# Blocks of 128 columns, paired writes of the transposed adjacency, and the last columns of eleven row tiles listed later

## The chip, the cores and the metric

The kernel runs on one core of one Trainium2 chip. The metric is the device time of one execution in microseconds; several runs of the same kernel are given by their median. The profile shows one execution, engine by engine: TensorE (PE, with its weight loads PEld), VectorE (DVE), ScalarE (ACT), GpSimd (POOL) and SyncE (SP), which here only starts DMAs.

## The reference

Four graph layers run one after the other on 2708 nodes with 128 features each. All use the same adjacency matrix `adj`, 2708 x 2708 in f32, symmetric in its pattern and with 0.6% of its entries other than zero; the diagonal is never zero. Every layer computes `x = x + layer(relu(layernorm(x)), adj)`.

```python
# layer 0
msg = adj.T @ h;  out = msg / adj.sum(axis=0)[:, None]
# layer 1
s, d = h @ W1[:, :D].T, h @ W1[:, D:].T
messages = gelu(s[:, None, :] + d[None, :, :] + msg_b)
aggregated = einsum('ijd,ij->id', messages, adj)
out = layernorm(gelu(concat([h, aggregated]) @ upd_w.T + upd_b) + h)
# layer 2: gru_cell(relu((adj @ h) @ W_msg.T + b_msg), h)
# layer 3: attention over the entries of adj, two heads
```

Layer 1 needs the message of a pair (i, j) only where `adj[i, j]` isn't zero. So the kernel makes lists of the nonzero entries of `adj`, and layer 1 works on the lists. Layers 2 and 3 need `adj` transposed (`adjT`), which is written to DRAM during layer 0.

## The kernel before, in words

**Tiles.** Rows are cut into 22 row tiles of 128 (the last has 20 rows), and these into six groups (`GROUPS`: five of four tiles, one of two). For layer 0 the columns are cut the same way into six column chunks c = 0 to 5. Chunks 0 to 4 have 512 columns of their own, the last (`LAST` = 5) has 148. A pair (c, s) of a column chunk and a row group is called a cut.

**Layer 0.** A loop goes through the 30 cuts of chunks 0 to 4, chunk after chunk and group after group within each (`order`). For each cut,

- `load_cut` (L320) loads the rows of the group from `adj` on SP's queue into one of five buffers `a` (`RING`). The load of the cut five places on is issued once the products of the cut have read its buffer. The last chunk has buffers `z0` to `z5` of their own, which are loaded during chunk 3.
- `list_cut` makes the lists on DVE. Columns are cut into blocks of `JB` = 124, 22 in all, the last with 104 columns. For each row tile and block, L360 finds the 8 largest values of each row, and L362 their column numbers in the block: one unit of work. A chunk's blocks 4c to 4c+3 begin at column 496c, so its window (`window`) begins before the chunk's own columns and is 512, 528, 544, 560 and 576 columns wide, and 228 for the last chunk.
- `mask_near` prepares on POOL the blocks that meet the diagonal (`near_blocks`, two of each row tile): L342 copies the block and L343 sets its diagonal to zero, since the entry on the diagonal is treated elsewhere.
- `work_cut` takes the four column tiles of the chunk in turn. For each, PE transposes the four row tiles (L406), ACT copies the result from PSUM to a buffer `aT` (L411, which sums the degrees on the way), and ACT's queue starts the write of the buffer of the turn before to `adjT` (L368, `write_one`; 128 rows of 512 columns, 256 KB). Then PE multiplies a row tile with the features (L392, `products`). `aT` has six buffers of 512 columns.

Between the cuts stand the small steps that turn the sums of earlier chunks into features of layer 1 (`turn_sums`, `turn_rows`, `destinations`, `add`, `measure`, `lift`; L255, L265, L435, L453, L464 and others). The parts of the last chunk are worked within chunk 4 (`PARTS`), and their lists (`list_last`) are spread: tiles 0 to 7 within chunk 4, tiles 8 to 13 after the last cut and ahead of `ends` (L635), tiles 14 to 16 ahead of `add(LAST)`, and tiles 17 to 20, of which only near blocks are listed here, among the steps ahead of layer 1.

**The lists that are made late.** For row tiles 17 to 20 (`LATER` to `NT - 2`) all but the near blocks, 80 units, are listed in layer 1's loop (`late_blocks`, `AT_ONCE` = 5 a period). The last row tile is listed there in a form of its own (`load_wide`, `list_wide`).

**Layer 1.** `period(t)` is executed for t = 0 to 22, with six steps k in each. PE multiplies the selected rows with selection matrices (L931, L935) and collects the results with the matrices `put` (L956); DVE prepares selection matrices (`columns`, L870 and L874; `select_rows` L776, `finish_rows` L787) and, in even periods, the sums for later tiles (`sources`, L900). At k = 4 SP issues the loads of the late blocks of the next period (`load_late`, into one of two buffers `cols_a`); at k = 1 DVE lists the first two (`EARLY`), at k = 5 the other three (`list_late`). The next period's steps follow behind these on DVE's queue.

The order of instructions on each engine is the order in which the program issues them. Waits between engines are derived from the buffers, and DMAs of SP and ACT take their semaphores from a common set in turn.

## Time and profile before

| what | value |
| --- | --- |
| time, median of 3 runs | 1015.22 us (1012.13 to 1015.25) |
| profiled execution | 1009.63 us |
| its span, first to last instruction | 1007.8 us |
| mean granted TensorE clock | 0.957 |
| PE busy | 912.5 us, 91% of the span |
| DVE busy | 795.9 us, 79% |
| ACT busy | 530.3 us, 53% |
| POOL busy | 461.4 us, 46% |
| read from DRAM, written | 117.26 MB, 30.87 MB |
| adjT writes of 256 KB on ACT's queue | 105 |

The busy time of an engine is the time in which it executed something. The shares are means over four layers that have different limits, so the page's slices (the span in 40 equal parts, each digit a busy share in tenths) are read first, then windows of the stage in question. The view of waits tells which engine stood still, which operation it was about to start, and what released it; a wait for several things is put down to the one that came last. A row of "DMA a<-in_adj" is a load of the adjacency into the ring of buffers, "adjT<-aT" a write of its transpose. Layer 0 fills the span up to about 200 us, the passage to layer 1 goes to about 245 us, and the first periods of layer 1's loop begin at about 250 us; period 1 begins at 262 us.

### The profile page before, as it was taken

What the parts mean: (1) busy time and instruction counts of PE and PEld (TensorE: products, weight loads), DVE (VectorE), ACT (ScalarE), POOL (GpSimd) and SP (SyncE); (2) the same over time, 40 slices, a digit from 0 to 9 for tenths busy, and PEclk for the clock granted to TensorE, in tenths of its full rate; (3) what the DMA queues carried; (4) which work ended last, traced back from release to release, by engine and by line L of the source; (5) the groups of instructions that cost most, each with busy time, mean ns of one, the idle gap of its engine ahead of it and who ended that gap; (6) DMA issues with size and microseconds to landing.
All of it is one profiled execution on the core that took longest, in us unless ns stands there. A gap on an engine that the chain in (4) does not pass through costs nothing. (4 is left out here: it accounts for less than half of the span.)

```text
span 1007.8 us, 22141 instructions
## 1 busy us (share of the span) xinstructions
PE 912.5 (91%) x7948; PEld 742.8 (74%) x7948; DVE 795.9 (79%) x2753; ACT 530.3 (53%) x1561; POOL 461.4 (46%) x588
## 2 busy tenths in 40 slices
PE   6799889945999999999999999999889999999983
PEld 3455455624999999999899744444678999999972
DVE  7999896976787898989966555676588977997793
ACT  5756557734666667667666324332322653564342
POOL 6413222424996779797966354443211300430142
PEclk9999999955999999999999899999899999999996
DMA  9999999422344334333322356654301574456000
GB/s 329 287 340 333 340 368 327 167 70 88 124 160 152 109 111 142 112 128 116 125 84 93 122 204 216 235 190 159 105 22 56 173 250 139 158 176 218 6 17 15
DMA packets 80458, 165.41 MB, mean 164 GB/s; under 512 B 9760, under 2 KB 25748, under 8 KB 80338
## 3 DMA queue, kind: packets, MB, share of 16 engines
q1 hardware_dynamic: 60358, 131.77, 39.7%
q10 hardware_dynamic: 19980, 32.14, 8.8%
q8 instruction: 64, 1.05, 0.4%
q14 instruction: 56, 0.46, 0.1%
HBM read 117.26 MB, written 30.87 MB: 147 GB/s over the span
## 5 line engine op out<-in xcount | busy, mean ns | idle before, releaser
L843 POOL TENSOR_SCALAR put<-count,line,value 128x128 f32<-128x128 f32 x176 | 199.7, 1146 | 10.9 <-PE agg L956 7.0
L1239 PE MATMUL att<-hv,wt 128*128 128x129 f32 x1672 | 196.0, 278 | 7.6 <-DVE wt L1209 6.2
L1239 PEld LDWEIGHTS att<-hv,wt 128*128 128x128 f32 x1672 | 192.2, 194 | 10.7 <-DVE wt L1209 8.7
L931 PE MATMUL p_m<-s,sel 128*128 128x128 bf16 x1452 | 162.3, 220 | 6.9 <-ACT g L943 4.6
L935 PE MATMUL p_m<-d,cols 124*128 124x128 bf16 (+1 forms) x1452 | 162.3, 220 | 3.9 <-DVE cols L874 3.9
L1209 DVE SCALAR_TENSOR_TENSOR wt<-row,lift,mask 128x1024 f32<-128x1024 f32 (+1 forms) x132 | 138.8, 1082 | 22.9 <-PE att L1239 22.9
L121 POOL TENSOR_TENSOR n_r<-n_r,minus_half 128x4 f32<-128x4 f32 (+1 forms) x28 | 39.6, 1413 | 243.5 <-DVE n_r L120 238.4
L956 PE MATMUL agg<-put,g 128*128 128x128 f32 (+1 forms) x968 | 123.5, 280 | 0.0
L392 PE MATMUL sums<-a,h 128*128 128x512 f32 x220 | 115.8, 622 | 1.6 <-ACT h L137 1.6
L956 PEld LDWEIGHTS agg<-put,g 128*128 128x128 f32 x968 | 114.2, 193 | 0.0
L406 PEld LDWEIGHTS p_T<-ident,a 128*128 128x128 f32 (+1 forms) x440 | 54.7, 144 | 77.1 <-issue 34.7
L931 PEld LDWEIGHTS <-sel 128*128 128x128 bf16 x1452 | 103.8, 98 | 8.6 <-issue 7.9
L1400 PE MATMUL p_agg<-a,hs 128*128 128x512 f32 (+2 forms) x264 | 107.7, 549 | 2.1 <-DMA a<-adjT 2.1
L935 PEld LDWEIGHTS <-cols 124*128 124x128 bf16 (+1 forms) x1452 | 102.8, 98 | 4.9 <-DVE cols L874 4.9
L943 ACT ACTIVATE g<-p_m 128x512 f32<-128x512 f32 x132 | 72.8, 553 | 59.4 <-PE agg L956 42.8
L852 ACT ACTIVATE put<-mine,value 128x128 f32<-128x128 bf16 x308 | 100.8, 393 | 0.0
L406 PE MATMUL p_T<-ident,a 128*128 128x128 f32 (+1 forms) x440 | 71.3, 283 | 24.6 <-ACT aT L411 18.0
L411 ACT ACTIVATE aT<-p_T 128x512 f32<-128x512 f32 (+2 forms) x132 | 71.0, 541 | 27.0 <-PE p_T L406 10.8
L1400 PEld LDWEIGHTS p_agg<-a,hs 128*128 128x128 f32 (+1 forms) x264 | 47.1, 191 | 49.2 <-issue 45.5
L362 DVE FIND_INDEX8 col<-val,a 128x8 uint16<-128x124 f32 x306 | 82.4, 281 | 0.0
L1362 ACT ACTIVATE hs<-hs 128x1354 f32<-128x1354 f32 (+1 forms) x44 | 58.4, 1329 | 39.5 <-DMA hs<-in_adj 39.1
L360 DVE MAX8 val<-a 128x8 f32<-128x124 f32 x306 | 70.9, 273 | 2.2 <-DMA a<-in_adj 2.2
(291 smaller groups left out, 1561.0 us busy)
## 6 DMA issues: line engine op xcount, KB each, us to landing
hs<-in_adj SPq DMA_DIRECT2D x42, 677.0 KB
adjT<-aT ACTq DMA_DIRECT2D x105, 256.0 KB
a<-adjT SPq DMA_DIRECT2D x20, 1280.0 KB
spread<-passed SPq DMA_DIRECT2D x22, 704.0 KB
later<-sel SPq DMA_DIRECT2D x22, 616.0 KB
a<-in_adj SPq DMA_DIRECT2D x5, 1152.0 KB
a<-in_adj SPq DMA_DIRECT2D x5, 1120.0 KB
a<-in_adj SPq DMA_DIRECT2D x5, 1088.0 KB
```

What stands on the lines that cost most here:

```text
L362: nc.vector.max_index(col[0:m, n, b, :], val[0:m, n, b, :], v)
L392: nc.tensor.matmul(accs[c][:, 0:w], h0[0:m, n, :], a[0:m, n - g0, t0 * P - lo : t0 * P - lo + w], start=(n == 0), stop=(n == NT - 1),)
L406: nc.tensor.transpose(p[0:k, i * iw + q * P : i * iw + q * P + m], a[0:m, q, e : e + k], ident[0:m, 0:m])
L843: nc.gpsimd.tensor_scalar(st["put", 0][:, b, :], count, st["line"][:, b : b + 1], st["value"][:, b : b + 1], ALU.is_equal, ALU.mult,)
L852: nc.scalar.activation(st["put", 1][:, b - HP, :], st["mine"][:, b - HP, :], AF.Identity, scale=st["value"][:, b : b + 1])
L931: nc.tensor.matmul(p[:, b - b0, :], st["sel"][:, b, :], s3[:, q, t % 2, :], start=(q == 0), stop=False)
L935: nc.tensor.matmul(p[:, b - b0, :], st["cols"][0:kb, b, :], d3[0:kb, b, q, :], start=False, stop=(q == 2))
L943: nc.scalar.activation(g[:, 0:n, :], state[t].pop(("p", k))[:, 0:n, :], AF.Gelu)
L956: nc.tensor.matmul(agg, g[:, b - 4 * k, :], put, start=(b == 0), stop=False)
L1209: nc.vector.scalar_tensor_tensor(wt[:, 0:n], row[:, k, c : c + n], lift[:, j, k : k + 1], mask[:, j, c : c + n], op0=ALU.max, op1=ALU.mult,)
L1239: nc.tensor.matmul(banks[s // 3][:, s % 3, :], wt[:, q * P : (q + 1) * P], hv[:, j, k, :], start=(v < 2 and s // 3 not in touched), stop=( ...
L1400: nc.tensor.matmul(pa[:, 0:n], h[0:k, j, :], a[0:k, j - j0, 0:n], start=(j == 0), stop=(j == NT - 1))
```

## The change

- Blocks are 128 columns wide. There are 22 still; the last has 20 columns. Windows are a chunk's own columns: 512, and 148 for the last. Each row tile has a single near block, its own (b = n), and `mask_near` has one multiply for it, on the cuts of the diagonal only.
- `late_blocks` leaves out b = n alone, which makes 84 units; the first four of them are cut off again (they are blocks 0 to 3 of tile 17, and are listed in layer 0), so 80 are left.
- The last 148 columns (blocks 20 and 21) of row tiles 6 to 16 (`HELD` to `LATER - 1`) are no longer listed in layer 0. `load_late` loads those of tile n for period n - 5, so in periods 1 to 11, with one more DMA of 128 x 148, and `list_late` at k = 5 lists them behind the other three units. The lists of tiles 0 to 5 are made in chunk 4: tiles 0 to 3 at group 1, tiles 4 and 5 at group 2. The two runs of `list_last` around `ends` and `describe` go, and of those among the steps ahead of layer 1 the two for tiles 20 and 21 are left, at the end.
- The parts of the last chunk share three buffers `z` in turn, in place of six. They are loaded at groups 3, 4 and 5 of chunk 3 and at groups 2 and 3 of chunk 4 (the last two together).
- A buffer `aT` holds 1024 columns, and there are five. The columns of two turns go into one buffer and are written with one DMA of 512 KB; parts of the last chunk, and the last row group, put as many into one as fit. A write is started, as before, at the next turn.

```diff
--- before.py
+++ after.py
@@ -41,7 +41,7 @@
 MASKED = -1e30
 FMAX = 3.4028234663852886e38
 
-JB = 124
+JB = P
 NB = (N + JB - 1) // JB
 S = 8
 E = P
@@ -192,11 +192,10 @@
     EARLY = 2
     WIDE = 4
 
-    def near_blocks(n):
-
-        return range(n * P // JB, (n * P + size(n) - 1) // JB + 1)
-
-    late_blocks = [(n, b) for n in range(LATER, NT - 1) for b in range(NB) if b not in near_blocks(n)]
+    late_blocks = [(n, b) for n in range(LATER, NT - 1) for b in range(NB) if b != n]
+    late_blocks = late_blocks[len(late_blocks) % AT_ONCE :]
+    HELD = 6
+    LAST_AT = {n - HELD + 1: n for n in range(HELD, LATER)}
     nc.gpsimd.memset(val[:, NT - 1, :, :], 0.0)
     nc.gpsimd.memset(col[:, NT - 1, :, :], 0.0)
 
@@ -285,7 +284,6 @@
 
     RING = 5
     BEHIND = 2
-    WINDOW = CH + 16 * (len(GROUPS) - 2)
     l0, ending = ExitStack(), ExitStack()
     ordered = ExitStack()
     lastp = ending.enter_context(tc.tile_pool(name="l0z", bufs=1, side="right"))
@@ -293,7 +291,7 @@
     once0 = l0.enter_context(tc.tile_pool(name="l0h", bufs=1))
     pool = l0.enter_context(tc.tile_pool(name="l0k", bufs=2))
     marked = l0.enter_context(tc.tile_pool(name="l0n", bufs=8))
-    turned = l0.enter_context(tc.tile_pool(name="l0t", bufs=6))
+    turned = l0.enter_context(tc.tile_pool(name="l0t", bufs=5))
     sump = l0.enter_context(tc.tile_pool(name="l0p", bufs=3, space=PSUM))
     turnp = l0.enter_context(tc.tile_pool(name="l0q", bufs=3, space=PSUM))
     h0 = once0.tile([P, NT, D], F32, name="h0")
@@ -305,16 +303,16 @@
 
     def window(c):
 
-        return 4 * JB * c, min(CH * (c + 1), N)
+        return CH * c, min(CH * (c + 1), N)
 
     def load_cut(c, s):
 
         g0, gk = GROUPS[s]
         lo, hi = window(c)
         if c < LAST:
-            a = rows_a.tile([P, 4, WINDOW], F32, name="a")
+            a = rows_a.tile([P, 4, CH], F32, name="a")
         else:
-            a = lastp.tile([P, gk, hi - lo], F32, name=f"z{s}")
+            a = lastp.tile([P, 4, hi - lo], F32, bufs=3, name="z")
         cuts[c, s] = a
         if gk == 4 and (c, s) != (0, 0):
             nc.sync.dma_start(
@@ -330,20 +328,13 @@
         g0, gk = GROUPS[s]
         lo = window(c)[0]
         a = cuts[c, s]
-        for n in range(g0, g0 + gk):
+        for n in range(g0, g0 + gk if c == s else g0):
             m = size(n)
-            for b in near_blocks(n):
-                if b // 4 != c:
-                    continue
-                e, k = b * JB, width(b)
-                e0, e1 = max(n * P, e), min(n * P + m, e + k)
-                p = lastp if c == LAST else marked
-                v = nears[n, b] = p.tile([P, JB], F32, name=f"near{n}_{b}" if c == LAST else "near")
-                nc.gpsimd.tensor_copy(v[0:m, 0:k], a[0:m, n - g0, e - lo : e - lo + k])
-                nc.gpsimd.tensor_tensor(
-                    v[0:m, e0 - e : e1 - e], a[0:m, n - g0, e0 - lo : e1 - lo],
-                    offdiag[0:m, e0 - n * P : e1 - n * P], ALU.mult,
-                )
+            p = lastp if c == LAST else marked
+            v = nears[n] = p.tile([P, JB], F32, name=f"near{n}" if c == LAST else "near")
+            nc.gpsimd.tensor_tensor(
+                v[0:m, 0:m], a[0:m, n - g0, n * P - lo : n * P - lo + m], offdiag[0:m, 0:m], ALU.mult
+            )
 
     def list_cut(c, s, n):
 
@@ -351,9 +342,9 @@
         lo = window(c)[0]
         units = []
         for b in range(4 * c, min(4 * c + 4, NB)):
-            if b in near_blocks(n):
-                units.append((b, nears.pop((n, b))[0:m, 0 : width(b)]))
-            elif n < LATER:
+            if b == n:
+                units.append((b, nears.pop(n)[0:m, 0:m]))
+            elif (n, b) not in late_blocks and n < (HELD if c == LAST else NT - 1):
                 units.insert(0, (b, cuts[c, s][0:m, n - GROUPS[s][0], b * JB - lo : b * JB - lo + width(b)]))
         for k in range(0, len(units), 2):
             for b, v in units[k : k + 2]:
@@ -396,6 +387,7 @@
 
         todo = list(range(g0, g0 + gk))
         js = list(range(t0, t0 + tk))
+        held = []
         turns = [js[q : q + 2] for q in range(0, tk, 2)] if gk < 4 == tk else [[j] for j in js]
         for js in turns:
             p = turnp.tile([P, CH], F32, name="p_T")
@@ -406,15 +398,21 @@
                     nc.tensor.transpose(
                         p[0:k, i * iw + q * P : i * iw + q * P + m], a[0:m, q, e : e + k], ident[0:m, 0:m]
                     )
-            aT = turned.tile([P, CH], F32, name="aT")
+            if not held:
+                aT = turned.tile([P, 2 * CH], F32, name="aT")
             for i, j in enumerate(js):
+                at = (len(held) + i) * iw
                 nc.scalar.activation(
-                    aT[0:k, i * iw : (i + 1) * iw], p[0:k, i * iw : (i + 1) * iw], AF.Copy, accum_out=degs[0:k, j, s : s + 1]
+                    aT[0:k, at : at + iw], p[0:k, i * iw : (i + 1) * iw], AF.Copy, accum_out=degs[0:k, j, s : s + 1]
                 )
             write_one()
-            written.append((
-                adjT[0:k, js[0] : js[0] + n, i0 : i0 + iw], aT[0:k, 0 : n * iw].rearrange("p (j i) -> p j i", j=n)
-            ))
+            held += js
+            if k < P or size(js[-1] + 1) < P or (len(held) + n) * iw > 2 * CH or js[-1] == t0 + tk - 1:
+                j, n = held[0], len(held)
+                written.append((
+                    adjT[0:k, j : j + n, i0 : i0 + iw], aT[0:k, 0 : n * iw].rearrange("p (j i) -> p j i", j=n)
+                ))
+                held = []
             for _ in range(2 if c == 0 else 1):
                 next(steps, None)
             if c > 0 and todo and gk == 4:
@@ -561,15 +559,17 @@
                 if c > 0 and s == (2 if c < LAST - 1 else 1) and n == g0 + 1:
                     invert(c - 1)
                 list_cut(c, s, n)
-            if c == LAST - 1 and 0 < s < LAST:
-                for n in range(2 * s - 2, 2 * s):
+            if c == LAST - 1:
+                for n in {1: range(4), 2: range(4, HELD)}.get(s, ()):
                     list_last(n)
         if i + 1 < len(order):
             mask_near(*order[i + 1])
         if i > BEHIND and i - 1 - BEHIND + RING < len(order):
             load_cut(*order[i - 1 - BEHIND + RING])
-        if c == LAST - 2:
-            load_cut(LAST, s)
+        for z in {(LAST - 2, 3): (0,), (LAST - 2, 4): (1,), (LAST - 2, 5): (2,), (LAST - 1, 2): (3,), (LAST - 1, 3): (4, 5)}.get(
+            (c, s), ()
+        ):
+            load_cut(LAST, z)
         if c > 0 and s == (2 if c < LAST - 1 else 1):
             turn_sums(c - 1)
         if (c, s) == (LAST - 1, LAST):
@@ -630,15 +630,11 @@
         split(*values_of(t), rest)
         describe_columns(t)
 
-    for n in range(8, 14):
-        list_last(n)
     nc.vector.tensor_copy(*ranked)
     for t in range(2):
         describe(t, d_rest[:, 2 * t : 2 * t + 2, :].rearrange("p q d -> p (q d)")[:, 0 : NB * S].rearrange(
             "p (b s) -> p b s", s=S
         ))
-    for n in range(14, 17):
-        list_last(n)
     add(LAST)
     measure(LAST)
     for _ in lift(LAST - 1):
@@ -710,7 +706,9 @@
             units = late_blocks[(t - 1) * AT_ONCE : t * AT_ONCE] if t > 0 else []
             if not units:
                 return
-            cols = work.tile([P, AT_ONCE, JB], F32, name="cols_a")
+            wide = N - LAST * CH
+            flat_cols = work.tile([P, AT_ONCE * JB + wide], F32, name="cols_a")
+            cols = flat_cols[:, 0 : AT_ONCE * JB].rearrange("p (b e) -> p b e", e=JB)
             state["late", t] = []
             for i, (n, b) in enumerate(units):
                 state["late", t].append((n, b, cols[0 : size(n), i, 0 : width(b)]))
@@ -728,6 +726,11 @@
                         adj[n * P : (n + 1) * P, b * JB : (b + k) * JB].rearrange("p (b e) -> p b e", e=JB),
                     )
                 i += k
+            if t in LAST_AT:
+                n = LAST_AT[t]
+                ends_of = flat_cols[:, AT_ONCE * JB :]
+                nc.sync.dma_start(ends_of, adj[n * P : (n + 1) * P, LAST * CH : N])
+                state["late", t] += [(n, NB - 2, ends_of[:, 0:JB]), (n, NB - 1, ends_of[:, JB:wide])]
 
         def list_late(t, first, last):
             units = state.get(("late", t), [])[first:last]
@@ -740,7 +743,8 @@
         pieces = [(b, min(WIDE, NB - 1 - b)) for b in range(0, NB - 1, WIDE)]
 
         def load_wide():
-            cols = state["wide"] = work.tile([P, AT_ONCE, JB], F32, name="cols_a")
+            cols = work.tile([P, AT_ONCE * JB + N - LAST * CH], F32, name="cols_a")
+            cols = state["wide"] = cols[:, 0 : AT_ONCE * JB].rearrange("p (b e) -> p b e", e=JB)
             for i, (b, k) in enumerate(pieces):
                 nc.sync.dma_start(
                     cols[i * TAIL : (i + 1) * TAIL, 0:k, :],
@@ -1114,7 +1118,7 @@
                 for g, step in updates.pop((t, k), ()):
                     update(g, step)
                 if k == GB - 1:
-                    list_late(t, EARLY, AT_ONCE)
+                    list_late(t, EARLY, None)
                     if now and NT - 2 <= t + 4 < NT:
                         count_rows(t + 4)
 
@@ -1132,12 +1136,12 @@
 
         puts = ExitStack()
         for step, n in (
-            (spread_ends, 0), (select_rows, 0), (rows, 5), (measure, 4), (turn_rows, 5), (list_last, 17),
+            (spread_ends, 0), (select_rows, 0), (rows, 5), (measure, 4), (turn_rows, 5),
             (finish_rows, 0), (fetch_both, 0), (spread_ends, 1), (select_rows, 1), (rows, 4),
-            (split_destinations, 3), (turn_rows, 4), (place, 0), (destinations, 4), (pass_on, 0), (list_last, 18),
+            (split_destinations, 3), (turn_rows, 4), (place, 0), (destinations, 4), (pass_on, 0),
             (finish_rows, 1), (fetch_both, 1), (split_destinations, 4), (destinations, 5), (spread_ends, 2),
             (select_rows, 2), (sources, 0), (sources_rest, 0), (describe_next, 2), (columns, 0), (place, 1), (split_destinations, 5),
-            *((list_last, n) for n in range(19, NT)),
+            (list_last, NT - 2), (list_last, NT - 1),
             (close_lists, 0),
         ):
             step(n)
```

## The prediction

> **What bounds the kernel now.** I began with the page's 40 slices (25.2 us each) to see where TensorE is not full.
>
> ```profile
> PE   6799889945999999999999999999889999999983
> DVE  7999896976787898989966555676588977997793
> PEclk9999999955999999999999899999899999999996
> DMA  9999999422344334333322356654301574456000
> ```
>
> Slices 1 to 7 are layer 0: DMA is at 9 and PE at 6 to 9. Slices 9 and 10 are the passage to layer 1: little DMA, half clock. From slice 11 PE is at 9. The change touches layer 0, the passage and the loop of layer 1 (to about 490 us), so I cut those open. Columns: length, busy time and count of PE, PEld, DVE, ACT, POOL, granted clock, DMA share, GB/s.
>
> ```profile
> 100.00:110.00 10.00, 7.67 (x33) 3.93 (x32) 10.00 (x65) 5.45 (x27) 1.27 (x1) 0.94 0.93 351
> 140.00:150.00 10.00, 9.12 (x41) 4.73 (x38) 7.79 (x52) 4.00 (x17) 2.94 (x5) 1.00 1.05 386
> 150.00:160.00 10.00, 8.30 (x34) 4.22 (x35) 1.44 (x11) 7.68 (x38) 3.64 (x9) 1.00 1.01 352
> 170.00:180.00 10.00, 10.00 (x67) 7.72 (x66) 10.00 (x69) 8.19 (x31) 3.31 (x9) 1.00 0.58 219
> ...
> 200.00:210.00 10.00, 7.96 (x21) 3.81 (x20) 5.54 (x32) 3.25 (x13) 2.21 (x6) 0.54 0.10 32
> ```
>
> Column chunks 1 to 3 (50.3 to 158.4 us by the last product of each) have DMA full; DVE is full but for about 14 us, most of it at 150 to 160, where it had no data. In chunk 4 (from 160) PE is full. What starves them is seen in the waits of 50 to 160 us (who waits, for whom: total, times, longest):
>
> ```profile
> SPq L320 <- PE sums L392: 65.8, 16, 7.1
> PEld p_T L406 <- ACT aT L411: 23.9, 24, 3.2
> PE p_T L406 <- ACT aT L411: 10.9, 9, 2.3
> ACT aT L411 <- DMA a<-in_adj: 8.5, 3, 3.8
> ACT junk L255 <- DMA a<-in_adj: 7.8, 3, 4.4
> ACT part_x L464 <- DMA a<-in_adj: 7.0, 2, 3.8
> ACT aT L411 <- DMA adjT<-aT: 5.7, 5, 3.2
> ```
>
> It is a ring. A load on SP waits for the products of five cuts earlier; PE waits for ACT to empty its transposes; ACT waits for a *load* of adj that its own operation doesn't read. ACT also issues the adjT writes (L368), and the loads and writes go round a small set of semaphores: a write stands behind the load that used its semaphore last. ACT stood still so for 11 gaps, 27.2 us in all, before 200 us (for instance 164.26 to 166.99, until the load issued at 158.4 landed), and 5.7 us for a write buffer.
>
> In the loop of layer 1 (262 to 404 us, then 418 to 470, same columns):
>
> ```profile
> 262.00:404.00 142.00, 141.74 (x2069) 140.36 (x2067) 120.12 (x319) 94.89 (x293) 115.15 (x122) 1.00 0.41 133
> ...
> 418.00:470.00 52.00, 50.83 (x747) 50.15 (x745) 47.09 (x144) 35.34 (x108) 44.89 (x47) 1.00 0.35 117
> ```
>
> PE bounds it; DVE has 22 us to spare in 142.
>
> **The change part by part.** The sum is made against the profiled execution: 1009.63 us, span 1007.8, 1.8 around it. It lies 5.6 us under the median of the runs, 1015.22; I carry my difference over to the median.
>
> *Load bytes.* Windows shrink from 512/528/544/560/576 and 228 columns to 512 and 148: 16+32+48+64+80 = 240 columns x 2708 x 4 B = 2.6 MB fewer. Some 2.4 MB of that falls in chunks 1 to 3, and the last columns of groups 3 to 5 (0.7 MB) load in chunk 4 instead, whose DMA share was 0.53 to 0.58. Before, 110 us moved
>
> ```profile
> DMA packets 22087, 38.02 MB, mean 346 GB/s; under 512 B 1515, under 2 KB 6015, under 8 KB 22074
> ```
>
> or 37.4 MB in 108.1 us; 34.3 MB are left. At the same 346 GB/s: 99.1 us, 9.0 less.
>
> *Paired adjT writes.* Four writes of 256 KB a cut become two of 512 KB. A round of eight semaphores, which five transfers a cut (one load, four writes) used up in 1.6 cuts, lasts 2.7 cuts, so a write is behind a load issued some 14 us ago and not 8. As built, about 27 writes of chunks 1 to 4 follow a load on its semaphore before and 16 after. I expect half or more of the 27 us of ACT stalls gone, and the stream fuller. How much rate does that give? In the 40 slices of that window the rate ran from 230 to 411 GB/s, and was low where one direction ran alone. The page "DMA: Bandwidth & Descriptors" of the Trainium skill (Bandwidth, "Where 436 GB/s comes from") says that transfers between HBM and SBUF are held by HBM at about 358 GB/s for a core: 34.3 MB then take 95.8 us, 12.3 less, and nothing more is to be had. The row above it, 386 GB/s over 10 us, contradicts that as a cap on reads and writes together; 375 would give 91.5 us, 16.6 less. What decides is therefore another engine. The buffers are 5 of 4 KB a partition for 6 of 2 KB: ten turns for six, but freed in pairs and later. If the pairs stall ACT as the single ones did (5.7 us), nothing is lost against now; that is why I don't book more than the following.
>
> *DVE in chunks 1 to 3.* From the lines by shape in the same 110 us:
>
> ```profile
> L362 DVE FIND_INDEX8 col<-val,a 128x8 uint16<-128x124 f32 x185 | 49.7, 280 | 0.0
> L360 DVE MAX8 val<-a 128x8 f32<-128x124 f32 x183 | 42.3, 271 | 2.2 <-DMA a<-in_adj 2.2
> ```
>
> A block costs about 0.445 us on DVE. Their number hardly changes here, and 4 columns more add some 8 ns a block (estimate, in proportion to the columns): 208 x 0.008 = 1.7 us. DVE was busy 96.0 of the 110 us; 97.7 after, 96 on the 108.1: so at most 12 less. PE's own work there is about 90. Three limits, 99.1 (bytes at the old rate), 96 (DVE), 91.5 (rate): I take 97, **-11**. Chunk 0 writes pairs too, but waits for its first loads: 0 to -2, I take -1. Chunk 4 is PE's pace (5.2 us a cut of its own work) and moves along: 0.
>
> *POOL.* One multiply for each diagonal tile replaces copies (0.29 us, 43 of them) and multiplies on two blocks a tile. POOL was busy 0 to 6.7 us of every 10: 0; not worth more, since nothing waited over 0.5 us for these.
>
> *Passage.* Before L635, DVE ran the lists of tiles 8 to 13, 194.15 to 199.26: 5.1 us, and PE (L453) waited 1.5 us for L635. They go. PE also arrives earlier, so not all 1.5 is won: -1. At 204.93 to 207.48 lists 14 to 16 stood before the addition of the last sums, while the last product ended at 205.8: -1.5 of 1.7. At 242.75, two near blocks of four less before the row selection: -0.5 of 0.9. Then the clock. It fell to half from 200.89 to 241.85, so the last cut's transposes and products took 1.97+4.08 us, against 2.18 for as many rows at full clock: 3.9 us more. The page "TensorE: Matmul & The Clock Gate" (Part 1: The HAM clock gate) lets the clock fall after about 3.4 us without work. By it the 1.5 us pause is too short to be the cause, and removing it wins none of the 3.9. The row says that PE was busy only 3.52 of the 5 us from 196 to 201, and the fall followed this stretch. I can't tell; between 0 and -3.9 I take -1. Passage: **-4**.
>
> *Loop.* Eleven periods (t = 1 to 11) each list two more blocks, 128 and 20 wide: 0.445 + about 0.23 = 0.68 us of DVE, 7.4 in all, at the end of a period, behind the attention values already made for it. Queued behind them are the next period's columns, which end 5 to 6 us before PE needs them, and in even periods the sums at L900 (0.69 us), for which PE paused 0.3 to 1.7 us at t = 8, 12 and 16. DVE's idle time in those periods is 0.45 to 3.4 us, 22.3 in all. Bounds: 0 (all hidden) and +7.4 (all shown). At t = 8 and near t = 11 and 12, where idle time is 0.45 to 0.5, the work can show: 0.7+1.4, so **+2**. One DMA of 74 KB more a period, at a DMA share of 0.41 and a whole period early: 0. The 80 blocks listed late for tiles 17 to 20 stay, four columns wider: 80 x 0.008 = 0.6 us, hidden.
>
> Sum: -1-11-4+2 = **-14**: 995.6 us profiled, 1001 as median.
>
> **The rivals.** *Bytes alone.* The semaphore waits only move: a 512 KB write takes longer than a 256 KB one, its buffer comes free later, ACT waits as before. Then layer 0 gains by bytes (-5.6 at the median time of a packet to -9.0), the passage -3, the loop +2: about -8, 1007 us. For it: ACT's waits for adj land on operations that the change doesn't touch (L255, L464). Against: half as many writes can stand behind a load.
>
> *All limits reached.* DVE follows without a hole and PE at its own pace, 90 to 92 us for chunks 1 to 3 with DVE's lag made good in chunk 4, where tiles 6 and 7 leave it (4 x 0.445); clock full to the last cut. -17-2-7+2 = -24: 991 us. Against it: DVE's 97.7.
>
> *Slower.* DVE becomes the bound of the loop: if what waits on the two late lists is the sums and columns of every period, all 7.4 us show, and an engine this near to full (120 of 142) loses again as much in bunching: +10 to +15. It decides once layer 0 gains less than that, that is if paired writes with five buffers stall ACT about 6 us more than now and eat the bytes. 1015+4 to 1015+8, say 1020. Against: idle 22 us where 7.4 are needed.
>
> *It doesn't do what it says.* The bytes go for certain. But if another ring (products free the load buffers, five cuts) sets the pace, the gain is given back in chunk 4: -2 with the loop, 1013.
>
> **How the numbers follow.** 0.3% of the time, 3 us, is about what a measurement here can tell from no change. My forecast (-10 to -18) 0.52, own range 997 to 1005; bytes alone 0.22; all limits 0.12; no effect 0.08; slower 0.06. Faster by over 0.3%: the first three and a fifth of the fourth, 0.88; same 0.06; slower 0.06. The range must hold 8 in 10: the forecast, bytes alone and the nearer part of the third: 992 to 1010.
>
> **What would show it.** Right: the ends of chunks 1 to 3 in 96 to 98 us; DVE without the hole at 150; the wait of ACT for adj loads below half; L635 at about 183 to 187 us; PE in the loop at 10 of 10 but for pauses at even periods, each below 2 us. Wrong: DMA share below 0.9 in chunks 1 to 3, ACT waiting for adjT writes over 10 us, SP waiting longer for PE, PE pausing for L900 or the columns in every period, or the half clock beginning earlier and lasting as long as the won time.

## The result, and the profile after

The changed kernel takes 1000.6 us (median of 6 runs, 995.61 to 1004.36); the kernel before, run beside it, 1012.6 us (6 runs, 1012.13 to 1015.25). The ratio is 0.9867 with a 95% interval of 0.9832 to 0.9901: 1.0 to 1.7% less. The profiled execution took 1000.98 us, with a span of 999.2; before, 1009.63 and 1007.8. Line numbers move a little: what was L360 and L362 (lists) is L351 and L353, L392 (products) is L383, L406 and L411 (transposes, their copies) are L398 and L405, L320 (ring loads) is L318, L368 (adjT writes) is L359, L255, L265 and L464 are L254, L264 and L462, L635 is L633, L931 and L935 are L935 and L939, L900 is L904.

The same four rows of the page's 40 slices, of the changed kernel:

```profile
PE   6799999757999999899899999999889999999983
DVE  8999999576988998879765656566588977997793
PEclk9999999758999999899999999999799999999996
DMA  9899997333454434243325266574201665556000
```

Slices 3 to 7 are now 9 on PE and DVE together. In slice 17 (400 to 425 us, in the loop of layer 1) PE and the clock show an 8 that wasn't there before.

I marked the stages by events that both traces have: the last product of chunk 0, of chunk 3, the first collecting matmul of the loop (L956, now L960) for tile 0 and for tile 21, and the end of the span.

| stage | before, us | changed, us | difference | predicted |
| --- | --- | --- | --- | --- |
| chunk 0 | 50.3 | 49.9 | -0.4 | -1 |
| chunks 1 to 3 | 108.1 | 94.2 | -13.9 | -11 |
| chunk 4 and the passage | 95.7 | 91.7 | -4.0 | -4 |
| loop, tile 0 to tile 21 | 305.6 | 312.8 | +7.2 | +2 |
| from there to the end | 448.1 | 450.6 | +2.5 | 0 |
| span | 1007.8 | 999.2 | -8.6 | -14 |

All rows are of one execution each. A second trace of the same changed kernel (below) has 94.9 for chunks 1 to 3, 310.7 for the loop and 447.6 for the rest, span 995.1. The stage from tile 21 to the end, which the change doesn't touch, thus differs by 3.0 us between two executions of one kernel, more than the +2.5 here, so I draw nothing from it.

Chunks 1 to 3 and the stage behind them, in windows (columns as before: length, busy time and count of PE, PEld, DVE, ACT, POOL, granted clock, DMA share, GB/s). First before, then changed:

```profile
50.30:158.40 108.10, 97.05 (x433) 54.89 (x434) 95.75 (x633) 63.97 (x245) 27.75 (x73) 0.98 1.00 346
158.40:254.10 95.70, 69.19 (x447) 48.80 (x447) 75.18 (x359) 52.90 (x181) 34.14 (x69) 0.75 0.42 148
```

```profile
49.90:144.10 94.20, 93.72 (x433) 54.97 (x434) 93.89 (x617) 65.03 (x241) 20.32 (x44) 1.00 1.03 355
144.10:235.80 91.70, 68.41 (x447) 48.27 (x447) 68.40 (x311) 53.11 (x181) 29.79 (x51) 0.76 0.49 171
```

DVE does nearly the same work in chunks 1 to 3 (95.75 and 93.89 us), but without holes: 0.3 us idle in 94.2. The DMA moves 33.4 MB at 355 GB/s, for 37.4 MB at 346. The waits of ACT in 50 to 145 us of the changed kernel (who waits, for whom: total, times, longest) name what went:

```profile
ACT aT L405 <- PE p_T L398: 16.6, 36, 2.0
ACT hs L137 <- POOL flat L275: 6.3, 3, 2.3
ACT d L247 <- DVE d_r L246: 4.3, 2, 2.6
ACT d L239 <- PE p_d L231: 2.1, 2, 1.1
ACT hT L152 <- PE p_h L150: 1.1, 2, 0.6
ACT junk L254 <- POOL xs L464: 0.7, 2, 0.3
```

No line names a DMA any more. Before, loads of adj held ACT for 27.4 us (8.5 + 7.8 + 7.0 + 4.1) and adjT writes for 5.7. ACT now waits for its own work, the transposes.

What those loads had to do with ACT stands in the trace of the kernel before. SP and ACT use eight semaphores between them. Each of the nine gaps of ACT for a load in 50 to 160 us ends with the start of a write (L368) on a semaphore that a load on SP had used last; the operation to which the wait is put down only follows it. The longest (start, duration, engine, line, operation, in brackets the idle time before it):

```profile
77.73 0.33 ACTq L368 DMA_DIRECT2D adjT<-aT  x1
78.10 0.31 ACT L255 ACTIVATE junk<-xs 128x128 f32<-128x128 f32 x1 [4.38 <-DMA a<-in_adj]
```

Of the 122 writes of the kernel before, 27 come after a ring load on their semaphore, at the median 8.3 us after that load was issued. With pairs 14 of 67 still do, at 11.6 us, and ACT stood for none of them in chunks 1 to 3.

The ring's loads on SP wait for DVE and no longer mostly for PE:

```profile
SPq L318 <- DVE col L353: 44.0, 10, 6.8
SPq L318 <- PE sums L383: 19.8, 10, 3.2
```

In the loop, DVE has 7.8 us more work in 142 us (127.89 for 120.12). PE stands still for 2.77 us at t = 12 (1.17 before), until ACT's `g` is ready, and the clock is at half for 6.8 us around it. The last line below is the stretch with t = 12:

```profile
246.00:388.00 142.00, 142.00 (x2046) 138.55 (x2045) 127.89 (x372) 94.72 (x291) 111.33 (x118) 1.00 0.45 138
...
402.00:454.00 52.00, 49.23 (x659) 47.78 (x657) 43.87 (x132) 32.92 (x100) 37.05 (x42) 0.93 0.34 104
```

From the first collecting matmul of one tile to that of the next, the plain periods, whose times recur all along the loop, take 14.44 and 13.58 us for 14.27 and 13.41 before: each 0.17 more. The period of t = 12 takes 21.29 for 16.64.

### The profile page after: what moved, and what is told of

It is laid out like the page before. It is cut to its first block, busy times and chain, and to the rows that moved or that the text cites. A ratio compares the mean times of both kernels' runs of the same rounds, so it can differ in the third digit from the quotient of the medians.

```text
span 999.2 us, 21970 instructions
## 1 busy us (share of the span) xinstructions
PE 915.4 (92%) x7948; PEld 743.3 (74%) x7948; DVE 796.8 (80%) x2753; ACT 532.8 (53%) x1561; POOL 444.3 (44%) x524
## 5 line engine op out<-in xcount | busy, mean ns | idle before, releaser
L847 POOL TENSOR_SCALAR put<-count,line,value 128x128 f32<-128x128 f32 x176 | 197.2, 1131 | 11.7 <-DVE value L836 11.7
L935 PE MATMUL p_m<-s,sel 128*128 128x128 bf16 x1452 | 162.5, 221 | 8.5 <-ACT g L947 6.2
L939 PE MATMUL p_m<-d,cols 128*128 128x128 bf16 (+1 forms) x1452 | 162.2, 221 | 3.8 <-DVE cols L878 3.8
L960 PE MATMUL agg<-put,g 128*128 128x128 f32 (+1 forms) x968 | 125.3, 282 | 0.0
L383 PE MATMUL sums<-a,h 128*128 128x512 f32 x220 | 115.5, 621 | 1.6 <-ACT h L137 1.6
L960 PEld LDWEIGHTS agg<-put,g 128*128 128x128 f32 x968 | 114.8, 194 | 2.4 <-issue 0.2
L935 PEld LDWEIGHTS <-sel 128*128 128x128 bf16 x1452 | 104.1, 99 | 10.1 <-issue 9.3
L939 PEld LDWEIGHTS <-cols 128*128 128x128 bf16 (+1 forms) x1452 | 101.9, 99 | 7.2 <-DVE cols L878 4.8
L398 PEld LDWEIGHTS p_T<-ident,a 128*128 128x128 f32 (+1 forms) x440 | 55.0, 143 | 61.0 <-issue 36.3
L353 DVE FIND_INDEX8 col<-val,a 128x8 uint16<-128x128 f32 x327 | 89.8, 287 | 0.0
L405 ACT ACTIVATE aT<-p_T 128x512 f32<-128x512 f32 (+2 forms) x132 | 71.1, 541 | 23.8 <-PE p_T L398 23.2
L398 PE MATMUL p_T<-ident,a 128*128 128x128 f32 (+1 forms) x440 | 70.0, 280 | 12.5 <-DMA a<-in_adj 6.2
L351 DVE MAX8 val<-a 128x8 f32<-128x128 f32 x327 | 77.6, 277 | 0.0
```

Of the source, the lines that this page charges most:

```text
L351: nc.vector.max(val[0:m, n, b, :], v)
L353: nc.vector.max_index(col[0:m, n, b, :], val[0:m, n, b, :], v)
L383: nc.tensor.matmul(accs[c][:, 0:w], h0[0:m, n, :], a[0:m, n - g0, t0 * P - lo : t0 * P - lo + w], start=(n == 0), stop=(n == NT - 1),)
L398: nc.tensor.transpose(p[0:k, i * iw + q * P : i * iw + q * P + m], a[0:m, q, e : e + k], ident[0:m, 0:m])
L847: nc.gpsimd.tensor_scalar(st["put", 0][:, b, :], count, st["line"][:, b : b + 1], st["value"][:, b : b + 1], ALU.is_equal, ALU.mult,)
L935: nc.tensor.matmul(p[:, b - b0, :], st["sel"][:, b, :], s3[:, q, t % 2, :], start=(q == 0), stop=False)
```

## The experiments

Times of each are compared with runs of the kernel before on the same chip, since chips and sets of runs differ by a few us. The stage columns come from the profile of each run.

| run | time, us | ratio to before, 95% interval | chunks 1 to 3 | loop |
| --- | --- | --- | --- | --- |
| changed kernel | 1000.6 | 0.9867 (0.9832 to 0.9901) | 94.2 | 312.8 |
| changed kernel again | 998.6 | 0.9863 (0.9835 to 0.9891) | 94.9 | 310.7 |
| single writes | 1008.7 | 0.9976 (0.9960 to 0.9992) | 101.7 | 311.6 |
| single writes, ten buffers | 1009.8 | 0.9973 (0.9953 to 0.9993) | 105.4 | 312.0 |
| single writes started by POOL | 1003.4 | 0.9921 (0.9896 to 0.9946) | 94.9 | 309.6 |
| windows and blocks alone | 1009.0 | 0.9979 (0.9963 to 0.9995) | 104.4 | 307.8 |
| lists back in layer 0 | 999.2 | 0.9898 (0.9867 to 0.9929) | 94.7 | 307.4 |
| tiles 6 to 9 back | 998.1 | 0.9886 (0.9857 to 0.9915) | 94.3 | 308.3 |
| padded last block | 993.3 | 0.9836 (0.9810 to 0.9861) | 94.9 | 307.1 |
| padded, tiles 6 to 9 back | 995.0 | 0.9836 (0.9802 to 0.9871) | 94.6 | 303.7 |
| padded, two lists later | 994.5 | 0.9843 (0.9800 to 0.9886) | 94.9 | 307.4 |
| padded, two lists later, tiles 6 and 7 back | 991.8 | 0.9828 (0.9779 to 0.9878) | 94.4 | 305.1 |
| padded, lists back in layer 0 | 997.2 | 0.9868 (0.9831 to 0.9904) | 94.4 | 304.3 |

**Which part makes layer 0 shorter.** First the writes alone were undone.

```diff
-    turned = l0.enter_context(tc.tile_pool(name="l0t", bufs=5))
+    turned = l0.enter_context(tc.tile_pool(name="l0t", bufs=6))
...
-                aT = turned.tile([P, 2 * CH], F32, name="aT")
+                aT = turned.tile([P, CH], F32, name="aT")
...
-            if k < P or size(js[-1] + 1) < P or (len(held) + n) * iw > 2 * CH or js[-1] == t0 + tk - 1:
+            if True:
```

> The changed kernel with one part undone: each turn's columns are written on their own again (256 KB, six buffers of 512 columns). Chunks 1 to 3 took 94.2 us with pairs and 108.1 us in the kernel before. Theory (the pairs take ACT off the loads' semaphores): ACT's waits for loads of adj come back by half or more, chunks 1 to 3 take 99 to 104 us, the time is about 1006 us (1004 to 1009). Rival (fewer bytes and the narrower windows do it alone): chunks 1 to 3 stay at 94 to 96 us and the time within 1.5 us of the changed kernel's 1000.6.

It takes 1008.7 us, and chunks 1 to 3 take 101.7. Most of the change's gain is gone with the pairs: 0.2% is left of 1.3%. ACT's waits in 50 to 160 us of this run:

```profile
ACT aT L405 <- DMA adjT<-aT: 8.3, 8, 1.5
...
ACT junk L264 <- DMA a<-in_adj: 6.3, 3, 3.3
...
ACT part_x L462 <- DMA a<-in_adj: 4.7, 2, 2.8
ACT junk L254 <- DMA a<-in_adj: 4.1, 2, 3.0
ACT aT L405 <- DMA a<-in_adj: 2.6, 1, 2.6
```

17.7 us for loads and 8.3 for writes are back. But six buffers of 512 columns also hold less than five of 1024. So the room was given back, with as many small writes; against the run before:

```diff
-    turned = l0.enter_context(tc.tile_pool(name="l0t", bufs=6))
+    turned = l0.enter_context(tc.tile_pool(name="l0t", bufs=10))
```

> The changed kernel with each turn's columns written on their own (256 KB), as in the run with single writes, but with ten buffers of 512 columns in place of six, so the columns held are as many as in the changed kernel (5 x 1024). Theory (the number of DMAs counts, since a write waits for the load that used its semaphore): ACT's waits for adjT writes (8.3 us with six buffers) go, those for loads of adj (17.7 us) stay at 12 us or more; chunks 1 to 3 take 98 to 102 us, the time is 1004 to 1008 us. Rival (the room in the buffers counts): chunks 1 to 3 take 94 to 96 us, the time is 999 to 1002 us.

1009.8 us, chunks 1 to 3 105.4. ACT's wait for adjT writes is gone, its waits for loads are 18.7 us in 50 to 160 us:

```profile
ACT junk L254 <- DMA a<-in_adj: 8.5, 3, 4.0
...
ACT part_x L462 <- DMA a<-in_adj: 5.2, 2, 2.6
ACT junk L264 <- DMA a<-in_adj: 5.0, 1, 5.0
```

The room in the buffers is not the cause. Either the number of DMAs is, by way of the semaphores that they share with the loads, or a DMA of 256 KB is slower than one of 512. The next run leaves number and size as they are and takes the sharing away: POOL starts the writes, and in its trace they use eight other semaphores than the DMAs of SP. It changes more than that: the writes go by another queue, in packets of 3.2 KB at the mean for 1.6, and ACT is rid of the 0.33 us that starting each one took it. Against the run with ten buffers:

```diff
-            nc.scalar.dma_start(*written.pop())
+            nc.gpsimd.dma_start(*written.pop())
```

> The changed kernel with single writes of 256 KB (ten buffers of 512 columns), started by POOL instead of ACT; POOL's writes have semaphores of their own as the program is built, so no write stands behind a load. Theory (what the pairs took away is ACT standing behind loads): ACT's waits for loads of adj, 18.7 us with single writes on ACT's queue, fall under 4 us though the writes are as small and as many; chunks 1 to 3 take 94 to 99 us, more than 94.9 only by what POOL's own work is delayed. Rival (256 KB writes are slower in themselves): chunks 1 to 3 stay at 102 to 106 us.

Chunks 1 to 3 take 94.9 us, the same as with pairs, and no wait of ACT for a load is left in 50 to 160 us. The bytes went at 362 GB/s, for 332 in the run with ten buffers. These are the lines of 50 to 145 us, first of the run with ten buffers on ACT's queue, then of that with POOL:

```profile
DMA packets 18997, 31.53 MB, mean 332 GB/s; under 512 B 1337, under 2 KB 4623, under 8 KB 18986
```

```profile
DMA packets 15431, 34.35 MB, mean 362 GB/s; under 512 B 1445, under 2 KB 3333, under 8 KB 15419
```

So writes of 256 KB need not cost anything in chunks 1 to 3, as far as that shows under the limit of DVE (busy 94.6 of 94.9 us). That they cost ACT its waits by way of the semaphores, and not by one of the other things that this run changes, is read from the trace of the run with ten buffers: each of its six gaps for loads, too, ends with the start of a write on a semaphore that a load on SP had used last.

As a whole the run is slower than the pairs (1003.4 us): its last cut ends at 193.3 us for 188 to 190, though the cut before ended no later (179.6 us). Its trace shows what holds it there. From 181.2 us POOL starts six writes in a row, 3.2 us. Behind them stand the diagonal tiles that POOL prepares for ACT (L379), for which ACT waits 2.0 us, and PE then waits 2.0 us for ACT. A write started by POOL takes 567 ns of POOL, here in 50 to 145 us (count, busy time and mean, idle time before and its releasers):

```profile
L359 POOL DMA_DIRECT2D adjT<-aT x64 | 36.2, 567 | 22.6 <-ACT aT L405 10.7 <-ACT part_x L462 8.0 <-ACT junk L254 2.0
```

**What the windows and blocks are worth alone.** Single writes with six buffers, as in the first of these runs, and all lists where they were (the last columns are still loaded where the change put them):

```diff
-    HELD = 6
+    HELD = 17
...
-            a = lastp.tile([P, 4, hi - lo], F32, bufs=3, name="z")
+            a = lastp.tile([P, 4, hi - lo], F32, bufs=6, name="z")
...
-                for n in {1: range(4), 2: range(4, HELD)}.get(s, ()):
+                for n in range(2 * s - 2, 2 * s) if 0 < s < LAST else ():
...
+    for n in range(8, 14):
+        list_last(n)
     nc.vector.tensor_copy(*ranked)
...
+    for n in range(14, 17):
+        list_last(n)
     add(LAST)
```

> Only the narrower windows and the blocks of 128 columns: the changed kernel with single writes (six buffers) and with the lists of tiles 6 to 16 back in layer 0 and the passage. Theory (the parts add up: single writes +8.1, lists back -1.4 against the changed kernel's 1000.6): 1006 to 1009 us; against the kernel before (1011.0 on this chip) 2 to 5 us less, in which 4 us are lost again in the loop to the 20-row matmuls. Rival (the windows make pairs worth having, so alone they do nothing): 1010 to 1013 us.

1009.0 us, 0.05 to 0.4% under the kernel before. Chunks 1 to 3 take 104.4 us, 3.7 less than before. The bytes of the stage fall from 37.4 to 34.5 MB, but the rate falls too, from 346 to 331 GB/s, for ACT's waits for loads are still 21.4 us. So fewer bytes by themselves bring little, though the share of the DMA was 1.00 before: a full share did not mean here that the DMA was the limit. Pairs with the old windows were not run; whether the windows make the pairs worth more stays open.

**What the late lists are worth.** The same edit of the lists, with the pairs kept; against the changed kernel it begins with

```diff
-    HELD = 6
+    HELD = 17
...
```

> The changed kernel with the lists of the last columns of tiles 6 to 16 back in layer 0 and the passage, where the kernel before has them (six buffers z). Blocks stay 128 wide, writes stay paired. Theory: the late lists cost the loop one long pause at t = 12 (2.8 us and a half clock behind it) and nothing in the other periods; so the 22 tiles of the loop take 307 to 309 us from first to last (312.7 changed, 305.6 before), and each plain period stays at 14.44 and 13.58 us; the passage is 3 to 6 us longer; the time is 999 to 1003. Rival (the late lists make every period 0.17 us longer): periods go back to 14.27 and 13.41, the loop to 305 to 306 us.

999.2 us, ratio 0.9898 with an interval that overlaps the changed kernel's. The loop starts 4 to 5 us later (first collecting matmul at 241.0 us, for 235.8 and 236.8 in the two traces of the changed kernel), and is 3.3 to 5.4 us shorter, with no pause of PE above 0.91 us at tiles 8 to 16. In the loop the late lists thus lose about what they win ahead of it; moving them is worth nothing that these runs can tell from zero. Plain periods stay at 14.44 and 13.58, so the 0.17 us has nothing to do with the lists.

Taking only tiles 6 to 9 back asks whether the lists of periods 8 to 11 make the long pause:

```diff
-    HELD = 6
+    HELD = 10
```

> The changed kernel with the last columns of tiles 6 to 9 listed in layer 0 too (at group 2 of chunk 4), so that the loop lists only seven tiles, in periods 1 to 7. DVE stood idle for 4.15 us ahead of L633 in the changed kernel; the eight blocks take 8 x 0.44 = 3.5 us less the narrow ones, about 2.8. Theory (DVE's lists in periods 9 to 11 make the pause at t = 12): layer 0 and the passage end as before the edit (within 1 us), the pause of PE at t = 12 falls from 2.8 to about 1.2 us without a half clock, loop 4 to 5 us shorter, 996 us. Rival (the pause stems from blocks of 128 or another order on DVE): it stays, and the time is the changed kernel's or up to 3 us more.

At t = 12 the period is 16.41 us, and PE pauses 0.89. That part of the theory holds. But t = 16 has a pause of 2.2 us and the half clock behind it (19.26 us for 17.0 to 17.8), and the loop begins 2 to 3 us later: the expected end of layer 0 and the passage "within 1 us" is wrong, though DVE had stood idle for 4.15 us ahead of L633. 998.1 us, the same as the changed kernel's 998.6.

**What makes every period longer.** In the changed kernel's trace, PE's matmuls at the end of a period (start, duration, engine, line, operation, tiles, shape, count) are these:

```profile
281.85 0.33 PE L939 MATMUL p_m<-d,cols 128*128 128x128 bf16 x3
282.02 0.33 PE L935 MATMUL p_m<-s,sel 128*128 128x128 bf16 x3
282.28 0.34 PE L939 MATMUL p_m<-d,cols 20*128 20x128 bf16 x3
282.55 0.49 PE L960 MATMUL agg<-put,g 128*128 128x128 f32 x2
```

Three matmuls start 0.17 us after the three before them. But the three over the 20 rows of the last block start 0.26 us after, and what follows them 0.27 us: single starts are 151 and 144 ns apart there, for 55. The weight loads show where the time goes. Elsewhere in this stretch the load for a matmul starts 2 ns after the matmul before it and is done alongside; the first load of 20 rows starts 147 ns after, 4 ns ahead of its own matmul, and the first load behind the 20 rows 142 ns after:

```profile
282.28 0.17 PEld L939 LDWEIGHTS <-cols 20*128 20x128 bf16 x3
```

Why such a load isn't started earlier the trace doesn't show. Before, the last block had 104 rows, and starts around it were 55 to 59 ns apart. With zeros below row 20, all matmuls of the loop can have 128 rows:

```diff
     d3 = fix.tile([P, NB, 3, D], BF16, name="d3")
+    nc.gpsimd.memset(d3[:, NB - 1, :, :], 0.0)
...
-                kb = width(b)
+                kb = P
```

> The changed kernel, but the last block's destinations are multiplied over 128 rows with zeros below row 20 instead of over 20 rows (three matmuls a tile). In the trace of the changed kernel the matmul that goes from 128 rows to 20 starts 151 ns after the one before and the one that goes back 144 ns, against 55 ns with 104 rows before. Theory (the change of rows costs about 0.09 us each way): plain periods fall from 14.44 to 14.25 to 14.28 us, the loop by about 4 us, the time to about 997. Rival (longer periods come from the lists or from blocks of 128): periods stay, no change.

Plain periods fall to 14.20 and 13.34 us, even under those of the kernel before, and the time to 993.3 us. The cause is shown: the three matmuls over 20 rows. Of the 0.24 us a period, the two late starts make 0.19 (151 + 144 - 2 x 55 ns). The pause at t = 12 is still there (2.98 us).

**Can the pieces be put together?** Padded, and tiles 6 to 9 back; against the padded kernel:

```diff
-    HELD = 6
+    HELD = 10
```

> Both edits that made the changed kernel faster together: last columns of tiles 6 to 9 listed in layer 0, and the last block's destinations padded with zeros to 128 rows. Theory (they act in different places, the pause at t = 12 and every period): the sum of both, 1000.6 - 7.3 - 2.5 = 991 us, 988 to 993. Rival (with shorter periods DVE falls behind elsewhere, at t = 8 or 16): 993 to 996 us.

995.0 us: the rival's time, but not by its reason. The loop is the shortest of all, 303.7, and t = 8 and 16 take 15.12 and 18.05 us, as in the padded kernel (15.12 and 17.86); but the loop begins at 241.4 us instead of 236.5. Next, padded, and the first two late lists of a period behind the last use of the sums on DVE:

```diff
                 if k == 1:
-                    list_late(t, 0, EARLY)
...
                     if now and t % 2 == 0 and t + 2 < NT:
                         sources_rest(t // 2 + 1)
+                    list_late(t, 0, EARLY)
```

> The kernel with the padded last block, and the first two late lists of each period moved on DVE from ahead of the sums (k = 1) to behind their last use (end of k = 2). In the padded kernel ACT waits at the start of period 12 for the sums and for v_r, 2.0 and 1.4 us, both behind these lists, and PE for ACT's g. Theory: the pause at t = 12 falls by the lists' 0.9 us, from 3.0 to about 2.1, that at t = 16 from 1.8 to about 0.9; the loop from 307.1 to 304 to 306 us, the time 991 to 993 us. Rival (DVE is behind by the whole backlog and what moves ahead is taken from the columns and rows of the next period): no change, 993 to 995.

994.5 us, the pause at t = 12 is 3.01 us, as it was. At t = 16 it falls from 1.77 to 1.30, and a later pause of that period grows from 0.51 to 1.34. The theory that these two lists delay what PE waits for falls. The rival fits: what moves on DVE's queue only changes places there. With fewer lists in the loop as well:

```diff
-    HELD = 6
+    HELD = 8
```

> As the run before it, and the last columns of tiles 6 and 7 listed in layer 0 too, so that the loop's extra lists end with period 9. DVE waited 4.1 us for L633 in the changed kernel, and the lists of two tiles take 1.4 us. Theory: layer 0 stays, the pause at t = 12 falls under 1.3 us with no half clock behind it: 3 us less than the padded kernel's 993.3, 989 to 992 us. Rival (what layer 0 takes over delays the passage as much, as with tiles 6 to 9): 992 to 995.

991.8 us, ratio 0.9828, the lowest, but the interval takes in that of the padded kernel, so that it isn't shown to be faster. The pause at t = 12 is 1.5 us and has no half clock behind it; 1.3 was expected. Last, padded with all lists of tiles 6 to 16 back in layer 0, by the edit of the lists shown above:

```diff
-    HELD = 6
+    HELD = 17
...
```

> The padded last block together with all lists of tiles 6 to 16 back in layer 0 and the passage: of the change only the windows, the blocks of 128 and the paired writes are left. Theory (moving the lists is worth nothing: layer 0 and passage give back what the loop loses): 992 to 995 us, as the padded kernel with the late lists (993.3); layer 0 and passage 4 to 5 us longer, loop 302 to 304 us with no pause over 1.3 us at t = 12. Rival (with the periods shorter, the late lists cost more than they bring): under 991 us.

997.2 us, 0.9868 against 0.9836 for the padded kernel with the late lists; the intervals overlap. The loop takes 304.3 us, with 1.4 us of pause at t = 12, and starts at 241.7: the stages are within half a us of what was expected, the time is 2 us above (on this chip the kernel before took 1012.4). Whether the late lists are worth 0 or 3 us is left open; they are not the reason for the gain.

The unaltered kernel for the comparison:

> The changed kernel unaltered, as the measure for its neighbours on the same chip. Expected: 999 to 1002 us; a long pause of PE and a half clock at t = 12 where the time is above 999.

998.6 us. Its trace has the pause at t = 12 (2.52 us) with 3.4 us of half clock behind it, where the first had 2.77 and 6.8 us; its period takes 19.66 us for 21.29. I had expected pause and half clock only in runs above 999 us; this one took 996.9.

## Why the prediction was right

By the sum, -14 was forecast and -12.0 came out between the two medians; 1001 us against 1000.6. That the two are so near is in part luck. Two errors went opposite ways: chunks 1 to 3 won 2 to 3 us more than the -11, and the loop lost 3 to 5 us more than its +2. And the kernel before came out at 1012.6 in six runs, 2.6 under the 1015.22 that I started from, which made up for the 2 us that the gain fell short. Of the signs that I had named, the hole of DVE, ACT's waits for loads and L633 at 183.5 us came as written; chunks 1 to 3 took 94.2 us and not 96 to 98, and PE's pause at t = 12 was not below 2 us.

*Paired writes.* The mechanism was as written: ACT stood behind loads because writes and loads share semaphores. Each of ACT's gaps for a load in the trace before shows it, and the run with POOL's writes, which took the sharing away among other things, had the gain in this stage whole. I had expected half or more of ACT's 27 us of waits to go; all went. And I had booked the gain mostly to the bytes (9.0 of 11, at an unchanged rate). That split was wrong: the windows alone bring 3.7 us in chunks 1 to 3 and 0.2% of the time, and undoing the pairs costs 7.5 us there and 8 us of the time, most of the change's gain. The rival *bytes alone* is refuted by the same runs, and so is its premise that waits at L255 and L464 can't be touched: they were waits of the write ahead of them on ACT's queue.

*The limit.* I named DVE as the limit of chunks 1 to 3, and it is: 93.89 of 94.2 us. Mis-sized was its work. I reckoned 97.7 us in a window of 110 and scaled that to 96 in the stage, though the stage before held 95.75 of DVE's work already, so that my own sum would have made it 97.4. It was 93.9, with 202 blocks in the stage for 206. A block cost some 12 ns more and not 8 (MAX8 and FIND_INDEX8 277 and 286 ns, for 271 and 280). PE, busy 93.72 us, is as close. The rate was 355 GB/s. The 358 of the Trainium skill's page "DMA: Bandwidth & Descriptors" ("Where 436 GB/s comes from") was thus not exceeded by the mean here, and by 1% with POOL's writes (362), while single slices of 2.4 us reach 408 (before 409, not the 411 that I had read). Since DVE was the limit in both, the runs don't show where that of the DMA lies.

*Passage.* -4.0, as summed, but not by each step. In the first trace 1.7 us of it lie ahead of the last product and 2.3 behind it, in the second trace 3.5 ahead, with 0.4 lost behind. The wait of PE for L633 fell from 1.5 to 0.4 us, for -1. The 1 us for the clock was a guess between 0 and -3.9, and in the first trace nothing came of it:

```profile
182.00:186.00 4.00, 3.58 (x20) 2.44 (x21) 0.23 (x1) 2.72 (x16) 0.00 (x0) 0.98 0.32 112
186.00:190.00 4.00, 3.84 (x4) 0.76 (x4) 1.76 (x6) 2.02 (x9) 1.66 (x5) 0.50 0.24 76
```

The pause had gone to 0.42 us, and the clock fell to half at 185.8 all the same, so that the last cut's products again took 4.06 us (4.08 before). In the second trace it fell at 191.5, behind the cut, which then took 8.5 us for 10.3. So removing the pause doesn't keep the clock, as I had inferred by the page "TensorE: Matmul & The Clock Gate" (Part 1: The HAM clock gate); but neither does that page's idle window explain a fall after 3.58 busy us of 4. What makes it fall here stays open.

*Loop.* The step that failed is "+2": it counted only DVE's pauses, and not the half clock that one of them brought. With and without the late lists and all else the same, the loops are 312.8 or 310.7 and 307.4 us, 311.6 and 307.8 with single writes, 307.1 and 304.3 when padded: the lists cost the loop 2.8 to 5.4 us. Left out was a term on PE: 0.17 us in each of some 21 periods against the kernel before, 3.6 us. Where the lists are back, 1.8 to 2.2 us of it are left in the loop as a whole (307.4 and 307.8 for 305.6), for there the pauses at t = 12 and 16 are shorter than before (0.9 us for 1.2 and 1.7). I had worked out what 128-wide blocks do to DVE and the DMA, and had not asked what a last block of 20 rows does to the matmuls that use it. The pause near t = 12 that I put at 1.4 us came, 1.4 to 1.6 us longer than before; the half clock behind it cost 1.5 to 3 us on top. With the matmuls over 20 rows that nearly makes my bound of +7.4, "all shown" (+7.2 and +5.1), by other means: most of DVE's 7.8 us stayed hidden.

The rival *slower* didn't come: it asked for ACT to stall on the five buffers, and ACT stalls on none.

## What to carry to other kernels

When an engine is recorded as waiting for a DMA whose data it doesn't read, look at what it starts itself: a DMA that it issues may stand behind another one's semaphore, and then fewer DMAs, or another engine to issue them, can free it, with hardly any byte saved. When a tile size is changed, work out the size of the last tile too and follow it to each engine that uses it: here a short remainder that costs VectorE less cost TensorE about 5 us, more than the whole move of the lists won. And an engine's idle time summed over a stage doesn't say that added work fits: 7.8 us of lists against 22 us of idle time still ended in a pause where the idle time had run out.

## What was not expected of the hardware

- A bf16 matmul over 20 rows started 151 or 152 ns after one over 128 rows instead of 55, each of ten times between 262 and 400 us, and the f32 matmul over 128 rows behind the last of them 144 or 145 ns after it. Matmuls over 104 and 124 rows showed no such step (55 to 60 ns).
- In all 14 traces the clock fell to half at the end of layer 0 or just behind it, and ahead of the first such fall PE had been idle for only 0.16 to 2.3 of 3.4 us, by its modelled busy time. In three of them it came back and fell again within 14 us. Nearly all stretches at half clock last a multiple of 3.4 us (3.4, 6.8, 10.2, 37.5). I found no rule in the traces for when it falls.
- Starting a write of 256 KB took ACT 326 ns and POOL 540 ns at the median (runs with ten buffers); with 256-KB writes from POOL the stage was as short as with 512-KB ones from ACT (94.9 and 94.2 to 94.9 us).
